# A gated cross-attention kernel on one Trainium2 core: a setup product split a second time, eight weight sums moved into the first quad, one buffer moved

## The chip, the cores and the metric

The kernel runs on one core of a Trainium2 chip. The metric is the time of one execution on the device in microseconds (us). The core's engines are named as the profile names them: PE is TensorE (matmul), PEld its weight loads, DVE is VectorE, ACT is ScalarE, POOL is GpSimd, SP is SyncE, which issues most DMAs. Each engine takes its own instructions in order and waits for the others by semaphores. PSUM, into which PE writes, has eight banks. SBUF is the working memory of all engines.

## The reference

`x` is (8, 1024, 1024), `ctx_1024` (the memory) is (8, 64, 512), all in float32. What is computed, with D = 1024:

```python
memory_proj = jnp.einsum('bme,de->bmd', memory, W_mem)
scores = jnp.einsum('bnd,bmd->bnm', hidden_states, memory_proj) / jnp.sqrt(jnp.float32(D))
attn = jax.nn.softmax(scores, axis=-1)
memory_context = jnp.einsum('bnm,bmd->bnd', attn, memory_proj)
gate_input = jnp.concatenate([hidden_states, memory_context], axis=-1)
gate = jax.nn.sigmoid(jnp.einsum('bnf,df->bnd', gate_input, W_gate) + b_gate)
fused = hidden_states + gate * memory_context
return _rmsnorm(fused, norm_w)
```

W_gate has two halves: W1 meets the rows of x, W2 meets memory_context. Since memory_context is attn times memory_proj, the kernel multiplies memory_proj by W2 once (the product "mg", 512 x 1024) and then attn by mg, so that the large product over all rows is x times W1 alone.

## The kernel before

**Strassen's products.** Each large product is done by Strassen's scheme in Winograd's form: the operands are cut into quarters, sums of quarters are formed, and seven products of quarters take the place of eight. The kernel numbers the seven products 1 to 7. The outer products run in the order 1, 6, 7, 5, 4, 2, 3 (`ORDER`, L604). In the main loop the scheme is used twice, one inside the other: each outer product is itself done by seven inner products, called A, B, C, D, A again, E and F (`outer_product`, L758). An inner product is two matmuls of 128x128 by 128x256, which the trace shows as four records.

**The rows.** x is worked in 16 quads of 512 rows (`NQ`). A quad has 49 slots (`SLOTS`), one for each inner product, and outer product number i of the order owns slots 7i to 7i + 6. The last two outer products of a quad are 2 (slots 35 to 41) and 3 (slots 42 to 48). Products 5, 4, 2 and 3 also carry the attn times mg part (`ext`, names pc and E, F).

**What is summed where.** The left sums of a quad, `outer_s` (DVE, 128x1024) and `inner_s` (POOL, four of 128x256 for each outer product, written to the tile L2), are made while the product before runs. The right sums come from W1 and are made once: `outer_sum` (L214, tiles t5, t6, t4) for products 5, 6 and 4, and `inner_sum` (L217, four of 128x512 for each outer product, tiles it1 to it7). The results are collected by `pre` on POOL (128x256 adds of u3 or u4, L797) and by `fin` on DVE (128x256 adds from PSUM, L803). `fin` of block n follows `pre` of block n.

**The banks.** An outer product uses five banks, and the next one takes them in rotated order (L898): its A gets the bank of the last product's C, its B that of D, its C that of A, its D that of E, its E that of B and F. So B of an outer product waits for the `fin` of D of the product before.

**The setup.** Before the first quad the memory is transposed and multiplied by W_mem (names pm, one step of Strassen), giving mp as the tiles m11 to m22. Then mg = mp times W2 follows in seven products of 256 x 512 by 512 x 512 (`mg_product`, L511: eight matmuls of 128x512 each, two banks; names pg) in the order 1, 6, 5, 2, 7, 4, 3. W2's quarters are b11 to b22, lists of four row chunks. The sums of mg are collected by DVE (`mg_sum`, L523) in c11, c12, c21 and c22, and stored to memory in DRAM (`store_mg`). Beside these products run: on POOL the sums of W2, then the inner sums of W1 for products 1, 7, 5, 6 and 4, with s3 (L540), s2 (L555) and `inner_s` of quad 0 between; on DVE the transposes of mp (`store_mp`, tiles mpq, stored to mgd by 16 DMAs), the transposes of xq, the outer sums of W1 and the sums of b21 (L569). The inner sums of products 2 and 3 are made by DVE in quad 0, at slots 3 to 6 and 22 to 25.

**Order.** Nearly every instruction is issued through `pin`, so each engine's queue has the order of the program text. Work that belongs to a later slot is put in by `at(slot, ...)`: what stands first in the program under one slot is issued first. `mid` puts work between A's second part and the `fin`s.

**Buffers.** The pool `const` has one buffer for each tag, `rot` two. A tile of the same tag has to wait until the accesses of the tile that held its buffer are over. Tag "l2" in `rot` is used by memq, then c21, then the L2 tiles. Tag "it2" in `const` is used by mpq of group 2 (`store_mp`, L492) and later by the inner sums of product 2; tags "it3" and "it4" likewise by mpq of groups 3 and 0 and by the inner sums of products 3 and 4.

These lines place the inner sums of products 2 and 3:

```python
for i, (o, n) in enumerate((o, n) for o in (2, 3) for n in range(4)):
    at((3, 4, 5, 6, 22, 23, 24, 25)[i], inner_sum, nc.vector, o, n)
```

Of the kernel before, what the change touches and what calls it, by code (L numbers as in the profile page):

```python
# [8 lines left out]
F32 = mybir.dt.float32  # L9
AF = mybir.ActivationFunctionType  # L10
ALU = mybir.AluOpType
# [4 lines left out]
P = 128  # L16
# [4 lines left out]
def tile_gated_cross_attention_rmsnorm(  # L21
# [42 lines left out]
    nc = tc.nc  # L64
# [8 lines left out]
    H = 512  # L73
    C = 256
# [4 lines left out]
    const = ctx.enter_context(tc.tile_pool(name="const", bufs=1))  # L79
# [3 lines left out]
    rot = ctx.enter_context(tc.tile_pool(name="rot", bufs=2))  # L83
    small = ctx.enter_context(tc.tile_pool(name="small", bufs=1))
# [4 lines left out]
    pin = tc.keep_in_program_order  # L89

    def mm(o, lhsT, rhs, start, stop):
        pin(nc.tensor.matmul(o, lhsT, rhs, start=start, stop=stop, skip_group_check=True))  # L92

    def tt(eng, o, a, b, op):
        pin(eng.tensor_tensor(o, a, b, op))  # L95
# [4 lines left out]
    def t4k(pool, shape, tag, name):  # L100
        return pool.tile(shape, F32, tag=tag, name=name)
# [5 lines left out]
    def chunks(t, n):  # L107

        return t.rearrange("p s e -> p (s e)").rearrange("p (m j) -> p j m", j=n)
# [26 lines left out]
    for k in range(KD):  # L136
        t = t4k(*((gpool, [P, D], "gate") if k < 7 else (apool, [P, D], "s4")), f"w2_{k}")
# [28 lines left out]
    def w1_place(o):  # L166

        if o in (5, 6, 4):
            outer_b[o] = const.tile([P, 4, H], F32, tag=f"t{o}", name=f"t{o}")
        inner_t[o] = const.tile([P, 3, 2, C], F32, tag=f"it{o}", name=f"it{o}")  # L170

    def w_op(o, s):
        if s >= T4:
            return inner_t[o][:, s - T4, :, :]
        k, n = {R11: (0, 0), R21: (1, 0), R12: (0, 1), R22: (1, 1)}[s]
        return outer_b[o][:, 2 * k : 2 * k + 2, n * C : (n + 1) * C]
# [37 lines left out]
    def outer_sum(o, a, b, k=slice(0, 4)):  # L214
        tt(nc.vector, outer_b[o][:, k], outer_b[a][:, k], outer_b[b][:, k], ALU.subtract)

    def inner_sum(eng, o, n):  # L217
        s, a, b = ((T1, R12, R11), (T2, R22, T1), (R12, R22, R12), (T4, R21, T2))[n]
        tt(eng, w_op(o, s), w_op(o, a), w_op(o, b), ALU.subtract)

    def inner_sums(eng, o):
        w1_place(o)
        for n in range(4):
            inner_sum(eng, o, n)
# [10 lines left out]
    def setup_bank(name):  # L235
        nonlocal setup_next
        tag = setup_banks[setup_next % 8]
        setup_next += 1
        return (ps_ctx if tag == "ctx" else ps).tile([P, H], F32, tag=tag, name=name)
# [8 lines left out]
    def pm_product(n, l, r, k_first=False):  # L248

        pgs = [setup_bank(f"pm{n}_{i}") for i in range(2)]  # L250
        if not isinstance(l, tuple):
            l = l[:, 0], l[:, 1]
        order = [(j, k) for j in range(KH) for k in range(2)]
        if k_first:
            order.sort(key=lambda jk: jk[1])
        for j, k in order:
            o = pgs[j // 2][:, (j % 2) * HM : (j % 2 + 1) * HM]
            mm(o, l[k][:, j, :], r[:, k, :], j % 2 == 0 and k == 0, k == 1)
        return pgs
# [34 lines left out]
    for k in range(2):  # L294
        pin(nc.scalar.copy(pw22[:, k], w22[:, k]))
    pgs = pm_product(2, w12, e21)
# [12 lines left out]
    pgs = pm_product(7, ps3, e12)  # L309
# [4 lines left out]
    b11, b12, b21, b22 = (  # L314
        [w2[h * KH + k][:, c * H : (c + 1) * H] for k in range(KH)]
        for h in range(2)
        for c in range(2)
    )
    t1, t2 = ([t[:, k, :] for k in range(KH)] for t in t_w2)

    def w2_sum(eng, o, a, b):
        for k in range(KH):
            tt(eng, o[k], a[k], b[k], ALU.subtract)
# [1 line left out]
    w2_sum(nc.gpsimd, t1, b12, b11)  # L325
    w2_sum(nc.gpsimd, t2, b22, t1)
    w2_sum(nc.gpsimd, b12, b22, b12)
    inner_sums(nc.gpsimd, 1)

    pgs = pm_product(3, ps4, e22)  # L330
    pm_sum(m21, m21, pgs)
# [8 lines left out]
    def transpose_x(q, t, half):  # L340

        key = q, t // 2, half
        if key not in A:
            A[key] = t4k(
                apool, [P, KH, 2 * P], f"a{t // 2 + 1}{half + 1}", f"a{t // 2 + 1}{half + 1}_{q}"
            )
        r = t % 2
        pin(
            nc.vector.transpose(  # L349
                A[key][:, :, r * P : (r + 1) * P],  # L350
                chunks(xq[q][:, 4 * t : 4 * t + 4, :], KD)[:, half * KH : (half + 1) * KH],
            )
        )

    def outer_s(q, n):
        a11, a12, a21, a22 = (A.get((q, r, h)) for r in range(2) for h in range(2))
        if n == 3:
            S[q, 3] = a21
            tt(nc.vector, a21, a11, a21, ALU.subtract)
            return  # L360
        s = S[q, n] = t4k(apool, [P, KH, 2 * P], f"s{n}", f"s{n}_{q}")
        if n == 1:
            tt(nc.vector, s, a21, a22, ALU.add)
        elif n == 2:
            tt(nc.vector, s, S[q, 1], a11, ALU.subtract)
        else:
            tt(nc.vector, s, a12, S[q, 2], ALU.subtract)
# [13 lines left out]
    def quarters(l):  # L381
        return l[:, 0:2, 0:P], l[:, 2:4, 0:P], l[:, 0:2, P:], l[:, 2:4, P:]
# [104 lines left out]
    def mp_step(eng, tag, pool, a, b, op):  # L487
        t = t4k(pool, [P, KH, HM], tag, f"mp_{tag}")
        tt(eng, t, a, b, op)
        return t  # L490
# [20 lines left out]
    def mg_product(n, l, r):  # L511
        pgs = []
        for t in range(2):
            pg = setup_bank(f"pg{n}_{t}")
            for k in range(KH):
                mm(pg, l[:, k, t * P : (t + 1) * P], r[k], k == 0, k == KH - 1)
            pgs.append(pg)
        return pgs

    def mg_tile(pool, tag, name):  # L520
        return t4k(pool, [P, 2, H], tag, name)

    def mg_sum(o, a, pgs):  # L523
        for t in range(2):
            tt(nc.vector, o[:, t, :], a[:, t, :], pgs[t], ALU.add)

    def store_mg(o, r, h):
        load(
            mgd[1, r * HM : (r + 1) * HM, h * H : (h + 1) * H].rearrange("(t p) e -> p t e", p=P),
            o,  # L530
        )

    s1 = mp_step(nc.vector, "s1", apool, m21, m22, ALU.add)
    s2 = mp_step(nc.vector, "s2", apool, s1, m11, ALU.subtract)
# [3 lines left out]
    outer_sum(7, 3, 7)  # L538
    w1_place(7)
    s3 = mp_step(nc.gpsimd, "junk", small, m11, m21, ALU.subtract)  # L540
    for n in range(4):
        inner_sum(nc.gpsimd, 7, n)
    c11 = mg_tile(rot, "u", "mg_c11")
    c12 = mg_tile(rot, "u", "mg_c12")
    c21 = mg_tile(rot, "l2", "mg_c21")
    c22 = mg_tile(small, "mg", "mg_c22")
    pgs = mg_product(1, m11, b11)
    for t in range(2):
# [4 lines left out]
    pgs = mg_product(6, s2, t2)  # L553
# [6 lines left out]
    pgs = mg_product(5, s1, t1)  # L560
    mg_sum(c12, c21, pgs)
    w1_place(6)
    outer_sum(6, 3, 5)
    for n in range(4):
        inner_sum(nc.gpsimd, 5, n)
    pgs = mg_product(2, m12, b21)
    mg_sum(c11, c11, pgs)
    store_mg(c11, 0, 0)
    w2_sum(nc.vector, b21, b21, t2)  # L569
    w1_place(4)  # L570
    outer_sum(4, 2, 6)
    for o in (6, 4):
        for n in range(4):
            inner_sum(nc.gpsimd, o, n)
    for t in range(2):
        transpose_x(0, t, 1)
    pgs = mg_product(7, s3, b12)
# [3 lines left out]
    pgs = mg_product(4, m22, b21)  # L581
    mg_sum(c21, c21, pgs)
    store_mg(c21, 1, 0)
    for t in (2, 3):
        transpose_x(0, t, 1)
    outer_s(0, 1)
    pgs = mg_product(3, s2, b22)
    mg_sum(c12, c12, pgs)
    store_mg(c12, 0, 1)
    outer_s(0, 2)  # L590
    load_mg(0)
# [5 lines left out]
    def at(slot, fn, *args):  # L597
        due.setdefault(slot, []).append(lambda: fn(*args))
# [45 lines left out]

    for o in (2, 3):
        w1_place(o)
    for i, (o, n) in enumerate((o, n) for o in (2, 3) for n in range(4)):
        at((3, 4, 5, 6, 22, 23, 24, 25)[i], inner_sum, nc.vector, o, n)
    slot = 0

    def step():
# [282 lines left out]
```

## Time and profile before

| what | us |
|---|---|
| median of 3 runs | 972.41 (972.2 to 973.52) |
| the profiled execution's own time | 972.56 |
| its span, first to last instruction | 970.8 |
| setup up to the first pg matmul | 0 to 33.44 |
| the seven products of mg (pg) | 33.44 to 81.5, PE busy throughout |
| quad 0, product 1 | from 81.35 |
| quad 0, product 6 | from 91.09 |
| quad 0, product 7 | from 97.45 |
| quad 0, product 5 | from 103.72 |
| quad 0, product 4 | from 111.89 |
| quad 0, product 2 | from 120.50 |
| quad 0, product 3 | from 128.67 |

The mean granted clock of TensorE over the span is 0.996 of full speed.

How to read the lines that follow in the prediction: a line of the timeline gives the start, the length in us, the engine, the line of the kernel, the operation and its tiles (output <- inputs), the shape, and how many instructions are merged; in brackets stands the idle time before it and who ended it. Most arithmetic is issued by two helpers, `mm` (L92) and `tt` (L95), so the tiles tell the operations apart and the lines don't. A line of the stretches gives the length and then busy us, with the number of instructions, of PE, PEld, DVE, ACT and POOL, the granted clock, the share of DMA and GB/s. A line of the waits gives the total, the number and the longest.

### The profile page before, as it was taken

The numbers are of one execution on the slowest core, as the hardware profiler recorded it, in microseconds if no ns is written. First come the engines' busy times: TensorE is split into PE (matmuls) and PEld (weight loads), VectorE is DVE, ScalarE is ACT, GpSimd is POOL, SyncE is SP. The second block draws the span as 40 slices with busy tenths as digits, with TensorE's granted clock in tenths as the row PEclk, the third lists the DMA queues.
The fourth block names the chain that finished last, engine by engine and source line by source line (L and its number), as shares of the span: only waits on it lengthen the run. The fifth ranks groups of instructions, "written<-read, shape, count | busy, mean of one in ns | idle before, by whom it ended". The sixth has DMA issues, their size and how long they took to land.

```text
span 970.8 us, 14402 instructions
## 1 busy us (share of the span) xinstructions
PE 959.5 (99%) x4986; PEld 774.9 (80%) x4986; DVE 818.4 (84%) x1482; ACT 328.5 (34%) x604; POOL 761.1 (78%) x889
## 2 busy tenths in 40 slices
PE   9999999999999999999999999999999999999995
PEld 8646878788888888788888888888887878888884
DVE  6988879879797988979797978979797978979787
ACT  2000234161423334161433324152333425152345
POOL 4997878778786978878786978878687878878692
PEclk9999999999999999999999999999999999999998
DMA  9856573482919374482918375381917465391712
GB/s 378 271 141 163 98 131 98 114 169 72 178 66 166 97 144 105 108 176 66 184 65 159 102 137 113 95 188 55 195 67 146 115 129 121 87 196 48 189 69 86
DMA packets 70919, 128.32 MB, mean 132 GB/s; under 512 B 12352, under 2 KB 49216, under 8 KB 70592
## 3 DMA queue, kind: packets, MB, share of 16 engines
q1 hardware_dynamic: 61520, 93.34, 37.0%
q0 software_dynamic: 9184, 33.56, 18.9%
q8 instruction: 39, 0.64, 0.3%
q10 hardware_dynamic: 144, 0.52, 0.1%
q14 instruction: 32, 0.26, 0.1%
HBM read 87.56 MB, written 41.68 MB: 133 GB/s over the span
## 4 chain that ended last, share of the span: by engine, by line
PE 98%; DVE 1%; issue 0%; ACT 0%; DVEq 0%
PE kA L92 20%; PE pc L92 12%; PE kE L92 11%; PE kD L92 10%; PE kF L92 10%; PE kB L92 10%; PE kC L92 10%; PE psT L92 6%; PE pg L92 5%; PE pm L92 3%; PE pz L92 0%; PE pa L443 0%; PE sc L417 0%; PE pt L196 0%; DVE gate L749 0%
## 5 line engine op out<-in xcount | busy, mean ns | idle before, releaser
L95 POOL TENSOR_TENSOR gate<-gate,u 128x256 f32<-128x256 f32 x336 | 287.5, 887 | 107.5 <-DVE u L95 107.5
L662 ACT ACTIVATE gate<-gate 128x512 f32<-128x512 f32 x128 | 80.5, 631 | 306.9 <-DVE gate L95 306.1
L349 DVE STREAM_TRANSPOSE a<-xq 128x512 f32<-128x512 f32 x128 | 137.9, 1099 | 2.7 <-POOL it L95 2.7
L95 POOL TENSOR_TENSOR l<-a 128x256 f32<-128x256 f32 x128 | 122.0, 953 | 21.6 <-PE kA L92 20.4
L92 PE MATMUL pc<-mg,attnT 64*128 64x256 f32 x512 | 127.5, 389 | 0.0
L92 PE MATMUL kB<-it,l 128*128 128x256 f32 x448 | 115.1, 379 | 0.2 <-DVE gate L95 0.2
L92 PE MATMUL kD<-it,l 128*128 128x256 f32 x448 | 115.0, 379 | 0.0
L92 PEld LDWEIGHTS pc<-mg,attnT 64*128 64x128 f32 x512 | 90.6, 186 | 29.9 <-issue 21.2
L691 DVE SCALAR_TENSOR_TENSOR gate<-gate,ss,nw_sb 128x512 f32<-128x512 f32 x120 | 110.6, 931 | 1.1
L95 POOL TENSOR_TENSOR l<-s 128x256 f32<-128x256 f32 x96 | 78.0, 813 | 36.1 <-PE kF L92 35.9
L92 PE MATMUL kA<-w,a 128*128 128x256 f32 x384 | 98.6, 379 | 0.0
L92 PEld LDWEIGHTS kB<-it,l 128*128 128x128 f32 x448 | 85.0, 190 | 12.1 <-DVE gate L95 0.6
L92 PEld LDWEIGHTS kD<-it,l 128*128 128x128 f32 x448 | 85.1, 190 | 11.6
L95 DVE TENSOR_TENSOR gate<-gate,pc 128x512 f32<-128x512 f32 x128 | 86.7, 678 | 0.4 <-ACT gate L662 0.4
L95 DVE TENSOR_TENSOR gate<-gate,kE 128x256 f32<-128x256 f32 x112 | 45.5, 419 | 47.1 <-PE kE L92 41.1
L92 PEld LDWEIGHTS kA<-w,a 128*128 128x128 f32 x384 | 71.7, 190 | 9.5 <-DVE s L95 0.2
L815 ACT COPY u<-kA 128x256 f32<-128x256 f32 x112 | 40.5, 361 | 110.3 <-PE kA L92 106.0
L92 PE MATMUL kE<-it,a 128*128 128x256 f32 x256 | 69.0, 392 | 0.0
L676 ACT ACTIVATE junk<-gate 128x1024 f32<-128x1024 f32 x60 | 63.5, 1058 | 10.5 <-DMA gate<-in_x 9.5
L92 PE MATMUL kA<-t,s 128*128 128x256 f32 x256 | 65.8, 379 | 0.0
L92 PE MATMUL kC<-w,l 128*128 128x256 f32 x256 | 65.7, 379 | 0.0
L92 PE MATMUL kF<-w,l 128*128 128x256 f32 x256 | 65.7, 379 | 0.0
(140 smaller groups left out, 2041.0 us busy)
## 6 DMA issues: line engine op xcount, KB each, us to landing
xq<-in_x SPq DMA_DIRECT2D x64, 512.0 KB, 10.3
gate<-in_x POOLq DMA_DIRECT2D x60, 512.0 KB, 8.1
out<-gate SPq DMA_DIRECT2D x60, 512.0 KB, 2.6
w<-in_w_gate_t SPq DMA_DIRECT2D x8, 512.0 KB, 10.0
w<-in_w_gate_t SPq DMA_DIRECT2D x2, 2048.0 KB, 17.1
mg<-mgd SPq DMA_DIRECT2D x16, 256.0 KB, 3.8
mpd<-mpT SPq DMA_DIRECT2D x4, 512.0 KB, 7.0
mgd<-mpq SPq DMA_DIRECT2D x16, 128.0 KB, 3.6
```

The costliest lines, as they stand in the source:

```text
L92: pin(nc.tensor.matmul(o, lhsT, rhs, start=start, stop=stop, skip_group_check=True))
L95: pin(eng.tensor_tensor(o, a, b, op))
L349: nc.vector.transpose(A[key][:, :, r * P : (r + 1) * P], chunks(xq[q][:, 4 * t : 4 * t + 4, :], KD)[:, half * KH : (half + 1) * KH],)
L662: pin(nc.scalar.activation(g, g, AF.Sigmoid))
L676: nc.scalar.activation(junk, O[q, t], AF.Square, accum_out=ss[:, t % 2 : t % 2 + 1])
L691: nc.vector.scalar_tensor_tensor(g[:, cols], g[:, cols], rstd[:, t % 2 : t % 2 + 1], nw_sb[:, cols], ALU.mult, ALU.mult,)
L815: pin(nc.scalar.copy(p1, kb["A"]))
```

## The change

Four things change.

- The last product of mp with W2, `mg_product(3, s2, b22)`, becomes `mg_nested`: the same product by a second step of Strassen. Its sums are four of b22's quarters for each of two row chunks (t1 to t4) and four of s2's (s1 to s4), twelve 128x256 operations on POOL. Seven products of 128x256 with two contraction steps follow on PE, in six banks. ACT copies the first, DVE makes u2, u3 and u4, POOL adds u3 or u4 to three blocks of c12, and DVE adds the four remaining banks. The sums lie in buffers it3 and it4.
- c21 moves from `rot`'s tag "l2" to `const`'s tag "it2".
- POOL's inner sums of products 5 and 4 leave the setup and come in quad 0 at slots 0, 0, 6, 6, 7, 7, 15, 15. The inner sums of product 1 on POOL come after s3's step.
- DVE's inner sums of products 2 and 3 move to slots 22 to 25 and 36 to 39.

```diff
     w2_sum(nc.gpsimd, b12, b22, b12)
-    inner_sums(nc.gpsimd, 1)
...
+    def mg_nested(eng, l, r, ts, ss, o):
+        l11, l12, l21, l22 = quarters(l)
+        s1_, s2_, s3_, s4_ = (ss[:, i] for i in range(4))
+        t1_, t2_, t3_, t4_ = (ts[i] for i in range(4))
+        lo, hi = slice(0, C), slice(C, H)
+        for k in range(2):
+            tt(eng, t1_[:, k, :], r[k][:, hi], r[k][:, lo], ALU.subtract)
+            tt(eng, t2_[:, k, :], r[2 + k][:, hi], t1_[:, k, :], ALU.subtract)
+            tt(eng, t3_[:, k, :], r[2 + k][:, hi], r[k][:, hi], ALU.subtract)
+            tt(eng, t4_[:, k, :], r[2 + k][:, lo], t2_[:, k, :], ALU.subtract)
+        tt(eng, s1_, l21, l22, ALU.add)
+        tt(eng, s2_, s1_, l11, ALU.subtract)
+        tt(eng, s3_, l11, l21, ALU.subtract)
+        tt(eng, s4_, l12, s2_, ALU.subtract)
+        yield
...
+        kb = [setup_bank(f"pn{i}")[:, :C] for i in range(6)]
+        ut = t4k(small, [P, 4, C], "junk", "mg_u")
+        p1_, u2, u3, u4 = (ut[:, i, :] for i in range(4))
+        def product(n, left_, right_, start=True):
+            for k in range(2):
+                mm(kb[n], left_[:, k, :], right_[k], start and k == 0, k == 1)
+        dst = [o[:, t, n * C : (n + 1) * C] for t in range(2) for n in range(2)]
+        def add(to, a, b):
+            tt(nc.vector, to, a, b, ALU.add)
+        product(0, l11, r11)
+        pin(nc.scalar.copy(p1_, kb[0]))
+        product(1, s2_, t2_)
+        add(u2, p1_, kb[1])
+        product(2, s3_, t3_)
+        add(u3, u2, kb[2])
+        for n in (3, 2):
+            tt(nc.gpsimd, dst[n], dst[n], u3, ALU.add)
+        product(3, s1_, t1_)
+        add(u4, u2, kb[3])
+        tt(nc.gpsimd, dst[1], dst[1], u4, ALU.add)
+        product(0, l12, r21, False)
+        product(4, l22, t4_)
+        product(5, s4_, r22)
+        yield
+        for n, b in ((0, 0), (3, 3), (2, 4), (1, 5)):
+            add(dst[n], dst[n], kb[b])
...
     s3 = mp_step(nc.gpsimd, "junk", small, m11, m21, ALU.subtract)
+    inner_sums(nc.gpsimd, 1)
...
-    c21 = mg_tile(rot, "l2", "mg_c21")
+    c21 = const.tile([P, 3, 2, C], F32, tag="it2", name="mg_c21")[:, :2]
+    c21 = c21.rearrange("p t k c -> p t (k c)")
...
     outer_sum(6, 3, 5)
-    for n in range(4):
-        inner_sum(nc.gpsimd, 5, n)
+    in_it3, in_it4 = (
+        const.tile([P, 3, 2, C], F32, tag=f"it{o}", name=f"mg_it{o}") for o in (3, 4)
+    )
+    ss3 = in_it4[:, 1:].rearrange("p a k c -> p (a k c)").rearrange("p (i k m) -> p i k m", i=4, k=2)
+    nested = mg_nested(
+        nc.gpsimd, s2, b22, [in_it3[:, 0], in_it3[:, 1], in_it3[:, 2], in_it4[:, 0]], ss3, c12
+    )
+    next(nested)
...
     outer_sum(4, 2, 6)
-    for o in (6, 4):
-        for n in range(4):
-            inner_sum(nc.gpsimd, o, n)
+    for n in range(4):
+        inner_sum(nc.gpsimd, 6, n)
...
     for t in (2, 3):
         transpose_x(0, t, 1)
+    next(nested)
     outer_s(0, 1)
-    pgs = mg_product(3, s2, b22)
-    mg_sum(c12, c12, pgs)
+    for _ in nested:
+        pass
     store_mg(c12, 0, 1)
...
+    for i, (o, n) in enumerate((o, n) for o in (5, 4) for n in range(4)):
+        at((0, 0, 6, 6, 7, 7, 15, 15)[i], inner_sum, nc.gpsimd, o, n)
     for i, (o, n) in enumerate((o, n) for o in (2, 3) for n in range(4)):
-        at((3, 4, 5, 6, 22, 23, 24, 25)[i], inner_sum, nc.vector, o, n)
+        at((22, 23, 24, 25, 36, 37, 38, 39)[i], inner_sum, nc.vector, o, n)
```

More of the change, by code (lines that the diff above doesn't have):

```diff
@@ L518, in mg_product @@
         return pgs
+    def mg_nested(eng, l, r, ts, ss, o):
[13 more added lines that the diff above has]
+        yield
+        r11, r22 = ([r[2 * h + k][:, n] for k in range(2)] for h, n in ((0, lo), (1, hi)))
+        r21 = [r[2 + k][:, lo] for k in range(2)]
+        t1_, t2_, t3_, t4_ = ([t[:, k, :] for k in range(2)] for t in (t1_, t2_, t3_, t4_))
+        kb = [setup_bank(f"pn{i}")[:, :C] for i in range(6)]
[24 more added lines that the diff above has]
+            add(dst[n], dst[n], kb[b])
     def mg_tile(pool, tag, name):
```

## The prediction

> **What bounds the kernel now.** I read the page's busy shares and chain first, then the waits of TensorE, then the stretches of the setup and the first quad, then each engine's timeline from 62 us to 131 us.
>
> ```profile
> PE 959.5 (99%) x4986; PEld 774.9 (80%) x4986; DVE 818.4 (84%) x1482; ACT 328.5 (34%) x604; POOL 761.1 (78%) x889
> ...
> PE 98%; DVE 1%; issue 0%; ACT 0%; DVEq 0%
> ```
> ```profile
> PE pz L92 <- DVE zeros L118: 1.2, 1, 1.2
> PE kB L92 <- DVE gate L95: 0.2, 1, 0.2
> ```
>
> TensorE is the bound: it is busy 959.5 of 970.8 us, and after its start it waits in the whole run only once, for 0.2 us. So all that can be won is TensorE work itself, and any new wait of TensorE is paid in full. That one wait is where the change reaches, in the first quad, so I look at who is loaded there.
>
> ```profile
> 62.13:81.98 19.85, 19.85 (x49) 9.03 (x48) 19.69 (x18) 0.00 (x0) 19.61 (x13) 1.00 0.21 79
> 81.98:87.64 5.66, 5.66 (x28) 4.72 (x28) 5.28 (x11) 0.74 (x2) 0.01 (x2) 1.00 0.60 179
> 87.64:103.59 15.95, 15.95 (x92) 13.03 (x91) 11.95 (x22) 3.00 (x8) 15.71 (x20) 1.00 0.87 152
> ```
>
> The columns are busy us of PE, PEld, DVE, ACT, POOL. POOL is full from 62.13 to 81.98 and from 87.64 to 103.59, with one hole of 5.65 us between. The next lines show both ends of this POOL queue, and what hangs on it.
>
> ```profile
> 73.46 1.27 POOL L95 TENSOR_TENSOR t<-t 128x512 f32<-128x512 f32 x1
> ...
> 79.73 2.25 POOL L95 TENSOR_TENSOR it<-t,it 128x512 f32<-128x512 f32 x1
> 87.64 0.91 POOL L95 TENSOR_TENSOR l<-s 128x256 f32<-128x256 f32 x1 [5.65 <-PE kF L92]
> ...
> 101.48 2.10 POOL L95 TENSOR_TENSOR gate<-gate,u 128x256 f32<-128x256 f32 x3
> ```
> ```profile
> 103.99 0.42 DVE L95 TENSOR_TENSOR gate<-gate,kF 128x256 f32<-128x256 f32 x1 [0.44 <-PE kF L92]
> ...
> 112.28 0.76 DVE L95 TENSOR_TENSOR gate<-gate,kD 128x256 f32<-128x256 f32 x2
> ```
> ```profile
> 113.09 1.13 PE L92 MATMUL kB<-it,l 128*128 128x256 f32 x4 [0.18 <-DVE gate L95]
> ```
>
> POOL's three `pre` adds of product 7 end at 103.59 (101.48 + 2.10). DVE's last `fin` of product 7 reads the third of them and starts at 103.99. From there DVE runs without a gap (attn_difference, four inner sums, u2 to u4, two transposes, the fins of product 5) to the kD fins, which end at 113.04, and TensorE's B of product 4, which reuses kD's bank, starts 0.05 us later. The chain POOL pre, DVE fin, DVE of product 5, TensorE has 0.4 us of slack at its head and none at its tail.
>
> **What the skill says.** "GPSIMD Engine Reference", section 1 Specifications: the SBUF interfaces are shared with VectorE, with contention where DVE has two SBUF inputs. The trace agrees: POOL's 128x512 sum takes 1.27 us alone (73.46) and 2.25 us beside DVE's 128x1024 outer_s (79.73). Section 4.1 Engine selection: two-input elementwise is about 2x slower on GpSimd. It agrees: 1.27 us against DVE's 0.68 us at 128x512. "PSUM — Partial Sum Buffer", section PSUM bank collisions: guard by bank, that is, a matmul waits for the reader of its bank. That is the 0.18 us wait at 113.09.
>
> **The change part by part.**
>
> TensorE. A product of mp with W2 takes 6.87 us (starts at 67.61, 74.48, 81.35). The nested one makes seven of 128x256 with two contraction steps each, 0.863 us apiece (four records; kA, kB, kC start 0.86 apart): 6.04 us. It removes 0.83 us, all of it on the path, if nothing it needs is late. Its sums come from POOL, in place of product 5's from 62.13 on: 12 x 0.69 = 8.3 us, plus 4.3 us beside DVE's four b21 sums (0.55 each, 1.71 - 1.27 and the issue) and its 128x2048 sum (2.1), so they end at 74.7, the tenth (s2_) at 73.3; the second nested product wants it at 75.3. Cover 2 us.
>
> POOL. Added in the setup: 8 sums of b22's quarters, 4 of s2's and 3 adds onto c12, all 128x256. Rows of that shape start 0.69 us apart (113.00, 113.69, 114.37): 15 x 0.69 = 10.35 us. Moved: 8 inner sums of products 5 and 4 (128x512) leave the setup and come at slots 0, 6, 7 and 15. They don't change the sum, since all eight stand ahead of product 7's `pre` in POOL's queue. W1's `inner_sums(1)` changes place with s3's step, both on POOL: s3 comes 5.0 us earlier, the sums 2.4 us later, and neither is needed before 60 us: nothing. The buffer of c21: rot's "l2" now serves only L2, so the wait of 5.65 us at 87.64 (for the F of product 1, which frees its buffer) goes, and slot 0's two sums fill the hole anyway. But outer_s(0,2) on DVE, 82.15 to 83.37, ran inside the hole; now POOL works beside it and loses about what 79.73 lost, 1.0 us. So the third `pre` of product 7 ends at 103.59 + 10.35 + 1.0 - 5.65 = 109.3. What is queued behind: L2's left sums for products 6, 7 and 5, b_gate's DMA, the `pre` adds of 6 and 7. Their fins on DVE free the banks for the next product's B and C, so TensorE stalls first at B of product 7, then at B of 5; all of that lies inside the final figure. DVE's last fin of 7 goes from 103.99 to about 109.35, +5.4. The DVE chain of product 5 is as long as before (four inner sums, now product 2's instead of 3's), so B of product 4 starts at 113.09 + 5.4 = 118.5. The 0.83 us won is swallowed: TensorE waits there whenever it came.
>
> DVE. In the setup two adds of 0.60 become seven of 0.33 (1.1 us more). dst[3], dst[2] and dst[1] wait for POOL's adds; behind them stand outer_s(0,2) and product 1's u2, which frees the bank for F of product 1. POOL: sums of product 6 to 80.7 (74.7 + 4 x 1.24 + 1.0 beside outer_s), adds to 82.8; so DVE's last add is done near 83.3, outer_s 84.7, u2 85.1; F wants the bank at 85.86. Covered by 0.8 us; if lost it lies in the same later wait. Slots 3 to 6 lose four inner sums (0.60 each), slots 22 to 25 swap them, slots 36 to 39, in product 2, get four new ones. There DVE is already without a gap from 120.77 to 128.5 (the four transposes, u's, pc's, fins). With four sums of 0.60 plus 0.5 us for a POOL sum that is under way at 121.7, the kD fin ends at 128.05 + 2.9 = 131.0; B of product 3 wants its bank at 129.53: a wait of 1.5 us. Bounds: 0.5 us (some of the 2.4 us falls into small gaps) to 2.9 us (DVE queues behind POOL as e did at 97.86, where a 0.4 us operation took 1.7). After it DVE idles 2.4 us at 137.4, so the backlog ends.
>
> c21 in it2. That buffer also holds mpq of group 2, whose stores land late (the longest of these is 9.6 us, the first issued at 43.3). DVE's add into c21 at 48.71 would wait to about 53.9. DVE idles 2.7 us there anyway for xq, so it is 2.4 us late afterwards; behind it are xq's transposes and b21's sums, which end at 67.74 and are wanted for the fourth chunk at 70.2. Hidden, at 0; bounds 0 and 2.4 us. c12's store and mg's load come up to 3 us later than 82.3 and 85.4; b_gate's DMA on POOL waits for mg and now issues at 98, and xq(1) behind it on SP lands near 102, wanted at 115: nothing.
>
> Sum: +5.4 (product 4) + 1.5 (product 3) = +6.9. Profiled span 970.8 + 6.9 = 977.7; around it lie 972.56 - 970.8 = 1.76, so 979.5, and the median is 0.15 under the profiled run: 979.3.
>
> The POOL term's bounds: 9.0 - 5.65 - 0.4 = 2.9 (adds at 0.6, no new contention) to 10.35 + 3.0 - 5.65 - 0.4 = 7.3 (two more DVE operations that cost POOL 1.0 each).
>
> **The rivals.**
> 1. POOL's backlog reaches TensorE, as above: 979.3, own range 975.8 (2.9 and 0.5) to 982.6 (7.3 and 2.9). Chance 0.70. For it: POOL's two full windows. Against: POOL's spans are rough.
> 2. Not slower. POOL absorbs the 15 adds. It decides at the third `pre` of product 7: if the net growth of POOL's queue stays under the 0.4 us of slack there, that is if adds plus contention cost at most 6.05 us, which the hole and the slack cover, where I count 11.35. Then the end is 972.41 - 0.83 = 971.6 up to 973.1 with the wait in product 3. For it: POOL's operations beside DVE hold long waits that could overlap. Against: alone they also take 0.69. Chance 0.12.
> 3. Half of it: POOL is late by 2 us only, because DVE's idle moments move away from POOL's sums, or the wait in product 3 is all that remains: 973 to 976, about 974.5. Chance 0.10.
> 4. More: c21's wait for its buffer delays DVE by 2.4 us and b21's sums come late for their product, and that lag goes on through product 1 into POOL: 979.3 + 2.4 to 4.5 = 981.7 to 983.8. Chance 0.08.
>
> **How the numbers follow.** This kernel's runs lie 0.14% apart, so 0.2% (1.9 us) is what can be told from no change. Case 2 is below 974.4 and mostly above 970.5: same 0.09, faster 0.03. A third of case 3 is within 974.4: same 0.12 in all, slower 0.85. The range 974.5 to 983.5 leaves out case 2, a third of case 3 and a little of case 4, about 0.18.
>
> **What would show it.** Right: no idle POOL between 82 and 88; the last `pre` of product 7 near 109; waits of kB in products 7, 5, 4 and 3, with B of product 4 about 5 us later than 113.09 and B of product 3 another 1.5 later; seven nested products in 6.0 us. Wrong: kB of product 4 at 112 to 113, TensorE without waits but the span near 970; or a wait of mg_c for mpq's DMA that TensorE feels in the setup.

## The result: 0.66% slower, and the profile after

| | before | after |
|---|---|---|
| median, us | 972.41 (972.2 to 973.52, 5 runs) | 978.75 (978.34 to 979.15, 5 runs) |
| ratio | | 1.0066, 95% interval 1.0054 to 1.0077 |
| span of the profiled execution | 970.8 | 977.0 |
| quad 0, product 1 (first kA) | 81.35 | 79.94 |
| product 6 | 91.09 | 89.88 |
| product 7 | 97.45 | 96.25 |
| product 5 | 103.72 | 108.11 |
| product 4 | 111.89 | 116.30 |
| product 2 | 120.50 | 125.37 |
| product 3 | 128.67 | 134.99 |
| quad 1, product 1 | 140.44 | 146.79 |

TensorE comes to the first quad 1.41 us earlier, and leaves it 6.35 us later. From there on the two run alike: the spans differ by 6.2. By stage: product 7 lasts 11.86 us instead of 6.27 (+5.59), and between the start of product 4 and that of product 3 it loses another 1.91 (18.69 against 16.78).

The page after, busy shares and chain:

```profile
PE 961.1 (98%) x4998; PEld 777.4 (80%) x4998; DVE 818.5 (84%) x1487; ACT 329.2 (34%) x605; POOL 775.0 (79%) x904
...
PE 90%; POOL 4%; DVE 3%; DMA 1%; issue 1%; ACT 0%; SPq 0%; DVEq 0%; POOLq 0%
```

POOL and DVE have entered a chain that was TensorE's for 98%. The waits of TensorE after (total, number, longest):

```profile
PE kB L92 <- DVE gate L95: 2.9, 2, 2.3
...
PE kD L92 <- DVE u L95: 0.8, 1, 0.8
PE pa L442 <- DVE e L95: 0.6, 1, 0.6
PE kC L92 <- POOL l L95: 0.4, 1, 0.4
```

Before there was one such wait, of 0.2 us. These waits are not all that TensorE loses. Of the 5.59 us lost in product 7, 3.31 are waits (2.26 at B, 0.44 at C, 0.61 at pa). The other 2.28 are matmuls that run longer: TensorE's busy time in product 7 (the first figure after the length) is 8.55 us instead of 6.27, with a mean granted clock (behind POOL's figure) of 0.86 instead of 1.00. The first line is before, the second after:

```profile
97.45:103.72 6.27, 6.27 (x32) 5.49 (x30) 4.73 (x10) 1.83 (x5) 6.19 (x10) 1.00 0.45 74
96.25:108.11 11.86, 8.55 (x31) 6.13 (x30) 7.82 (x11) 1.84 (x5) 11.70 (x16) 0.86 0.43 69
```

In the stretch in which C runs, right behind the waits at B and C, the granted clock was 0.58. The prediction has no such term. In the kernel after, the end doesn't hang on it: it lies ahead of B of product 4, and this B still waits 0.63 us for DVE.

The same three stretches as before, and the new one up to the end of product 7's `pre`:

```profile
62.13:81.98 19.85, 19.85 (x66) 12.11 (x65) 19.71 (x25) 0.75 (x2) 19.62 (x18) 1.00 0.21 80
81.98:87.64 5.66, 5.66 (x34) 4.24 (x34) 4.66 (x9) 0.37 (x1) 5.50 (x6) 1.00 0.46 146
87.64:103.59 15.95, 13.25 (x66) 10.10 (x63) 10.33 (x13) 1.53 (x4) 15.79 (x16) 0.93 0.91 163
103.59:109.15 5.56, 4.95 (x22) 3.83 (x21) 4.16 (x8) 1.47 (x4) 5.48 (x9) 0.89 0.00 0
```

POOL (the fifth busy figure) is full in all four; the hole of 5.65 us is gone. What fills it, on POOL's timeline:

```profile
79.44 3.08 POOL L95 TENSOR_TENSOR mg_c<-mg_c,mg_u 128x256 f32<-128x256 f32 x3
82.48 1.27 POOL L95 TENSOR_TENSOR it<-t 128x512 f32<-128x512 f32 x1
83.82 2.14 POOL L95 TENSOR_TENSOR it<-t,it 128x512 f32<-128x512 f32 x1
85.92 0.73 POOL L95 TENSOR_TENSOR l<-s 128x256 f32<-128x256 f32 x1
...
88.79 2.25 POOL L95 TENSOR_TENSOR t<-t 128x512 f32<-128x512 f32 x1
...
101.43 1.51 POOL L95 TENSOR_TENSOR t<-t 128x512 f32<-128x512 f32 x1
102.65 1.51 POOL L95 TENSOR_TENSOR it<-t,it 128x512 f32<-128x512 f32 x1
...
107.05 2.10 POOL L95 TENSOR_TENSOR gate<-gate,u 128x256 f32<-128x256 f32 x3
```

The three adds onto c12, then two of product 5's inner sums at slot 0, L2 for product 6 from 85.92 (87.64 before), four more sums from 88.79, two at 101.43, and the `pre` adds of product 7 end at 107.05 + 2.10 = 109.15. DVE's last `fin` of product 7 follows at 109.19:

```profile
100.73 4.40 DVE L95 TENSOR_TENSOR e<-e,den 128x256 f32<-128x256 f32 x1
...
109.19 0.42 DVE L95 TENSOR_TENSOR gate<-gate,kF 128x256 f32<-128x256 f32 x1 [0.26 <-POOL gate L95]
```

And TensorE, at B of products 7 and 4 and at the attn times mg part of product 2:

```profile
99.53 1.13 PE L92 MATMUL kB<-it,l 128*128 128x256 f32 x4 [2.26 <-DVE gate L95]
...
117.96 1.13 PE L92 MATMUL kB<-it,l 128*128 128x256 f32 x4 [0.63 <-DVE gate L95]
...
132.53 0.70 PE L92 MATMUL kD<-mg,attnT 64*128 64x256 f32 x2 [0.76 <-DVE u L95]
```

The nested products start at 73.90 and end where product 1 starts, at 79.94: 6.04 us.

### The profile page after: what moved, and what is told of

It reads as the page before. It is cut to its first block, busy times and chain, and to the rows that moved or that the text cites. A ratio compares the mean times of both kernels' runs of the same rounds, so it can differ in the third digit from the quotient of the medians.

```text
span 977.0 us, 14451 instructions
## 1 busy us (share of the span) xinstructions
PE 961.1 (98%) x4998; PEld 777.4 (80%) x4998; DVE 818.5 (84%) x1487; ACT 329.2 (34%) x605; POOL 775.0 (79%) x904
## 4 chain that ended last, share of the span: by engine, by line
PE 90%; POOL 4%; DVE 3%; DMA 1%; issue 1%; ACT 0%; SPq 0%; DVEq 0%; POOLq 0%
PE kA L92 19%; PE pc L92 12%; PE kE L92 11%; PE kD L92 10%; PE kF L92 10%; PE kB L92 10%; PE kC L92 10%; PE psT L92 6%; PE pm L92 2%; DMA xq<-in_x 1%; POOL it L95 1%; POOL mg_it L95 1%; POOL l L95 1%; PE pz L92 0%; DVE e L95 0%
## 5 line engine op out<-in xcount | busy, mean ns | idle before, releaser
L751 DVE SCALAR_TENSOR_TENSOR gate<-gate,ss,nw_sb 128x512 f32<-128x512 f32 x120 | 108.3, 912 | 1.1
```

Of the source, the lines that this page charges most:

```text
L751: nc.vector.scalar_tensor_tensor(g[:, cols], g[:, cols], rstd[:, t % 2 : t % 2 + 1], nw_sb[:, cols], ALU.mult, ALU.mult,)
```

## The experiments

The theory put to the test: what stands in POOL's queue ahead of product 7's `pre` adds sets their end (T below), T sets DVE's stretch of product 5, and this sets B of product 4; four DVE sums in product 2 add some 1.4 us. Each kernel was timed beside the kernel before on the same chip (972.2 to 972.3 there).

| run | median, us | ratio (95%) | T | B of 4 | B of 4 less T | span |
|---|---|---|---|---|---|---|
| before | 972.4 | | 103.59 | 113.09 | 9.5 | 970.8 |
| after | 978.75 | 1.0066 (1.0054 to 1.0077) | 109.15 | 117.96 | 8.8 | 977.0 |
| e1 plain product | 976.37 | 1.0039 (1.0026 to 1.0052) | 105.86 | 114.70 | 8.8 | 973.7 |
| e2 sums earlier | 979.74 | 1.0073 (1.0059 to 1.0086) | 109.56 | 119.06 | 9.5 | 978.1 |
| e3 c21 back | 978.95 | 1.0067 (1.0054 to 1.0079) | 108.69 | 118.17 | 9.5 | 977.2 |
| e4 DVE sums back | 979.83 | 1.0077 (1.0065 to 1.0090) | 111.05 | 120.53 | 9.5 | 978.0 |
| e5 no b22 sums | 979.92 | 1.0081 (1.0067 to 1.0095) | 109.89 | 118.71 | 8.8 | 977.7 |
| e6 before plus 4 | 972.31 | 1.0001 (0.9993 to 1.0009) | 103.41 | 112.89 | 9.5 | 970.6 |
| e7 before plus 15 | 981.67 | 1.0096 (1.0083 to 1.0110) | 112.25 | 122.16 | 9.9 | 979.7 |
| e8 product 3's sums in product 4 | 977.75 | 1.0056 (1.0043 to 1.0069) | 108.95 | 118.44 | 9.5 | 976.0 |
| e9 nested alone | 982.16 | 1.0101 (1.0087 to 1.0115) | 113.62 | 123.08 | 9.5 | 981.4 |
| e10 no c12 adds | 977.27 | 1.0049 (1.0035 to 1.0062) | 107.64 | 117.31 | 9.7 | 976.5 |
| e11 sums spread | 974.92 | 1.0032 (1.0021 to 1.0042) | 102.82 | 113.34 | 10.5 | 973.0 |
| e12 sums spread again | 972.32 | 0.9999 (0.9990 to 1.0007) | 103.46 | 112.89 | 9.4 | 970.8 |

**The two halves apart.** e1 takes the nested product out of the kernel after and keeps the moves; e9 puts the nested product alone into the kernel before (its sums in it2 and it3).

```diff
# e1, from after
-    nested = mg_nested(...)
-    next(nested)
...
+    pgs = mg_product(3, s2, b22)
+    mg_sum(c12, c12, pgs)
# e9, from before
+    nested = mg_nested(...)
+    next(nested)
     for n in range(4):
         inner_sum(nc.gpsimd, 5, n)
...
-    pgs = mg_product(3, s2, b22)
-    mg_sum(c12, c12, pgs)
```

> Kernel after, with only the nested product undone: mg_product(3, s2, b22) again, all moved sums and c21's buffer as after. Theory A (GpSimd's fifteen added 128x256 operations, 10.35 us, are what makes product 7's pre adds late): the third pre of product 7 ends near 99 to 100 instead of 109.15, no wait in products 7, 5 and 4; TensorE gets 0.83 us more work back and the 1.4 us of product 2 stay: span 970.8 + 1.4 = 972.2, about 973.9 us. Theory B (the eight moved inner sums make it late by standing between product 6's and 7's work): still 977 to 979.

> Kernel before, with the nested product as the only change: its sums in it2 and it3, c21 in l2, every inner sum where it was before. GpSimd then makes the sums of products 5, 6 and 4 between the nested sums and the adds onto c12, which so start near 89 us; DVE and product 1's F wait for them. Theory A3 (the end of product 7's pre adds is what counts, and the nested product and the moved sums are two ways to the same delay): L2's sums for product 6 start near 93, the third pre of product 7 ends at 109 to 110, about 978; no wait in product 2. If the moved sums are to blame: 971.6 to 973.

Neither half is free: the moves alone cost 4.1 us of time (T 2.3 later), between the two expectations for e1, and the nested product alone 10.0, well above the expected 978. In e1 POOL now idles in the setup, and the sums that would fit there stand in the quad. Its timeline:

```profile
72.91 1.27 POOL L95 TENSOR_TENSOR it<-t,it 128x512 f32<-128x512 f32 x1
82.77 0.73 POOL L95 TENSOR_TENSOR l<-s 128x256 f32<-128x256 f32 x1 [8.59 <-DVE s L95]
```

L2 of product 6 can't start before DVE's outer_s ends, however empty POOL's queue is. In e9 the wait sits elsewhere. The waits of TensorE in e9, and the POOL line behind them:

```profile
PE kF L92 <- DVE u L95: 8.6, 1, 8.6
```
```profile
90.33 2.09 POOL L95 TENSOR_TENSOR mg_c<-mg_c,mg_u 128x256 f32<-128x256 f32 x3
```

The c12 adds stand behind the sums of products 5, 6 and 4 in POOL's queue and come at 90.33 instead of 79.44. DVE's c12 adds wait for them, and behind those stands product 1's u2, which frees the bank of F. Product 1 lasts 20.96 us instead of 9.74, which is 2.6 us more than the wait: its matmuls run longer here too, with a mean granted clock of 0.76. So in e9 TensorE is late from product 1 on, and T is late with it.

**The sums moved only part of the way.** e2 makes product 5's sums in the setup, ahead of product 6's, and product 4's at slot 0.

```diff
-    for n in range(4):
-        inner_sum(nc.gpsimd, 6, n)
+    for o in (5, 6):
+        for n in range(4):
+            inner_sum(nc.gpsimd, o, n)
...
-    for i, (o, n) in enumerate((o, n) for o in (5, 4) for n in range(4)):
-        at((0, 0, 6, 6, 7, 7, 15, 15)[i], inner_sum, nc.gpsimd, o, n)
+    for i, (o, n) in enumerate((o, n) for o in (4,) for n in range(4)):
+        at((0, 0, 0, 0)[i], inner_sum, nc.gpsimd, o, n)
```

> Kernel after, with product 5's inner sums on GpSimd back in the setup (ahead of product 6's) and product 4's all at slot 0; the nested product stays. Theory A (the amount of work ahead of product 7's pre adds counts, not its place): their end stays near 109, the time stays at 978.7 within 1.0. Theory B (the place of the eight sums counts): 971.6 to 974.

T is 0.4 us later (109.56) and the time 1.0, at the edge of what the first theory allowed. The wait has moved from product 7 to F of product 1 (4.2 us, again for DVE's u), and product 1 lasts 7.3 us longer than before, at a mean granted clock of 0.80. All eight sums stood ahead of product 7's `pre` in both; so far that is what the prediction's sum of the queue says.

**The added operations.** e6 and e7 add 4 and 15 subtractions of b22's quarters (128x256), whose results nothing uses, to POOL's queue at the end of the setup of the kernel before. e5 leaves out of the kernel after the eight sums of b22's quarters (the nested product then takes the raw quarters, so c12 is another matrix). e10 leaves out the three adds of u3 and u4 onto c12.

```diff
# e6, e7, from before
+    extra = t4k(small, [P, C], "extra", "extra")
+    for i in range(4):   # 15 in e7
+        tt(nc.gpsimd, extra, b22[i % 4][:, :C], b22[i % 4][:, C:], ALU.subtract)
# e5, from after
-            tt(eng, t1_[:, k, :], r[k][:, hi], r[k][:, lo], ALU.subtract)
...
-            tt(eng, t4_[:, k, :], r[2 + k][:, lo], t2_[:, k, :], ALU.subtract)
# e10, from after
-            tt(nc.gpsimd, dst[n], dst[n], u3, ALU.add)
...
-        tt(nc.gpsimd, dst[1], dst[1], u4, ALU.add)
```

> Kernel before, with 4 more 128x256 subtractions on GpSimd (2.8 us) into a tile that nothing reads, at the end of the setup's queue. They lie in the hole of 5.65 us: unchanged within 0.5. If GpSimd's work is paid for everywhere: 2.8 us slower.

> Kernel before, with 15 such subtractions (10.35 us) at the same place, as many as the change adds. Theory A: the hole takes 5.65, the slack at product 7 0.4, DVE's outer_s and four inner sums now meet a busy GpSimd (up to 1.0 + 2.2): between 4.3 and 7.5 us slower, the third pre of product 7 at 108.3 to 111.5, with no change of the product, the buffer or any slot.

> Kernel after, with the eight sums of b22's quarters left out: the nested products multiply b22's quarters themselves, so that mg is another matrix, and TensorE's work is unchanged. GpSimd loses 8 x 0.69 = 5.5 us. Theory A in its first form (every us taken from GpSimd comes back): third pre of product 7 at 103.7, about 974. Theory A2 (GpSimd can't run ahead of outer_s(0,2), which it needs near 82.7, so that only the excess over that comes back, as in the kernel with the plain product): pre near 105.9, 3.0 us faster than after, about 975.7.

> Kernel after, with the three adds of u3 and u4 onto c12 left out on GpSimd (2.1 us), so three blocks of c12 lack them. Theory A3 (these adds wait for DVE's u3 near 79.2 and hold up GpSimd's queue, so that sums ahead of them are free and work behind them is not): L2's sums for product 6 start 1.5 us earlier (bound then by outer_s(0,2)), 1.5 us faster than after, about 977.2. Theory A in its first form: 2.1 faster. If work ahead of product 6 is all free: 978.7.

Four operations vanish in the hole. Fifteen took 16.10 us (1.07 each, not 0.69), pushed L2 of product 6 to 97.20, and cost 9.4 us, more than the 4.3 to 7.5 expected:

```profile
81.14 16.10 POOL L95 TENSOR_TENSOR extra<-w 128x256 f32<-128x256 f32 x15
```

TensorE waited 7.2 us at B of product 6, and this product lasted 10.1 us longer than before, at a mean granted clock of 0.69. In e5 eight operations of 0.69 less gave nothing back, where both expectations had 3 us or more. POOL's timeline in e5 shows why:

```profile
73.12 1.28 POOL L95 TENSOR_TENSOR it<-t,it 128x512 f32<-128x512 f32 x1
80.23 3.07 POOL L95 TENSOR_TENSOR mg_c<-mg_c,mg_u 128x256 f32<-128x256 f32 x3 [5.83 <-DVE mg_u L95]
83.26 1.26 POOL L95 TENSOR_TENSOR it<-t 128x512 f32<-128x512 f32 x1
```

The c12 adds wait for u3, which TensorE and DVE have only then (mg_u starts at 79.24 on DVE, 78.44 after), and hold all that is queued behind them: POOL idles 5.83 us where the sums were. T is 0.74 us later than after, about as much as DVE's mg_u. e10 is the counterpart: without those three adds POOL goes from product 6's sums at once to slot 0's, and of the 2.1 us that they take alone (2.09 in e9) 1.5 come back in T, and 1.5 in the median time; POOL then waits 1.41 us for DVE's outer_s ahead of L2 of product 6, which hides the rest. In the profiled execution of e10, the slowest of its five (978.24), B of product 4 starts only 0.65 us earlier than after and waits for nothing: there TensorE comes last, held in product 7 by DVE's e, an operation that the last section comes back to:

```profile
PE pa L442 <- DVE e L95: 2.2, 1, 2.2
```

So an operation ahead of that wait costs nothing until the queue ahead lasts past it, and one behind it makes T later, up to what the next wait hides.

**The moved buffer and DVE's moved sums.** e3 puts c21 back into "l2". e4 puts DVE's sums back to slots 3 to 6 and 22 to 25, e8 moves product 3's from product 2 into product 4.

```diff
# e3
-    c21 = const.tile([P, 3, 2, C], F32, tag="it2", name="mg_c21")[:, :2]
-    c21 = c21.rearrange("p t k c -> p t (k c)")
+    c21 = mg_tile(rot, "l2", "mg_c21")
# e4, e8: slots of DVE's sums of products 2 and 3
-(22, 23, 24, 25, 36, 37, 38, 39)
+(3, 4, 5, 6, 22, 23, 24, 25)     # e4
+(22, 23, 24, 25, 32, 32, 33, 34) # e8
```

> Kernel after, with c21 back in the two-buffer tag l2. Theory A: DVE's wait of 5.67 us at 48 us for mpq's stores shrinks to the 2.7 us for xq, but it is hidden either way, and slot 0's sums cover the wait for product 1's F: 978.7 within 0.7. Theory C (c21's wait delays DVE and so everything behind it): 976.3 or less. Theory D (the buffer is what fills GpSimd's hole): slower by up to 1.5.

> Kernel after, with DVE's inner sums of products 2 and 3 back at slots 3 to 6 and 22 to 25. Theory A: the 1.2 us wait in product 2 goes, but the four sums at slots 3 to 6 now meet a busy GpSimd and cost it up to 0.55 us each: between 977.3 (no contention) and 979.5 (all four). If the slots of these sums cost nothing: 978.7.

> Kernel after, with DVE's four inner sums of product 3 at slots 32, 32, 33, 34 in place of 36 to 39: DVE idles there 2.8 us in four pieces. Theory A: the wait in product 2 (about 1.4 us) goes and nothing takes its place: 977.3. If the sums only move the lag to product 4: 978.7.

e3 can't be told from after. In e8 TensorE's wait for kD in product 2 is gone (A of product 2 to A of product 3 takes 8.29 us, 9.62 after), for 1.0 us of time. In e4 it is gone too (8.16), but the sums at slots 3 to 6 run beside POOL's L2 of product 6 (1.18 and 1.06 us an operation, 0.73 after), T is 1.9 us later, and the time 1.1 above after, just outside the expected range.

**Another place for the sums.** e11 and e12 keep the whole nested product and c21's buffer and change only the inner sums of products 5, 4, 2 and 3: their slots, and which of the two engines makes them. (In the lists: slot, product, n.)

```diff
# e11
+        (nc.gpsimd, ((0, 5, 0), (0, 5, 1), (22, 5, 3), (22, 4, 2), (27, 4, 3), (37, 3, 0), (41, 3, 1), (41, 3, 2), (44, 3, 3))),
+        (nc.vector, ((3, 4, 0), (4, 4, 1), (5, 5, 2), (22, 2, 0), (23, 2, 1), (32, 2, 2), (33, 2, 3))),
# e12
+        (nc.gpsimd, ((0, 5, 0), (0, 5, 1), (23, 4, 2), (27, 4, 3))),
+        (nc.vector, ((3, 4, 0), (4, 4, 1), (5, 5, 2), (6, 5, 3), (22, 2, 0), (23, 2, 1), (24, 2, 2), (32, 2, 3),
+                     (32, 3, 0), (33, 3, 1), (34, 3, 2), (46, 3, 3))),
```

> Kernel after, with the inner sums of products 5, 4, 2 and 3 spread anew: on GpSimd two of product 5 at slot 0 and one at 22, two of product 4 at 22 and 27, product 3's at 37, 41, 41, 44; on DVE two of product 4 and one of product 5 at slots 3 to 5, product 2's at 22, 23, 32, 33. The six sums of 1.24 us that stand between product 6's left sums and product 7's pre adds go, three on DVE cost GpSimd up to 0.55 each. Theory A3: the third pre of product 7 ends near 103.5, no wait above 0.5 us in products 7, 5, 4 and 2, and the 0.83 us of the nested product is left over: 970.5 to 972.5. If the nested product's sums themselves are what is paid: still 976 or more.

> After with the sums of products 5, 4, 2 and 3 spread once more: GpSimd makes only four in the quad (two of product 5 at slot 0, one of product 4 at slots 23 and 27), VectorE the other twelve (slots 3 to 6, 22 to 24, 32 to 34 and 46). Theory (what stands in POOL's queue between its wait for the nested u3 and the third pre of product 7 sets B of product 4, and each engine's other work decides the rest): POOL carries 2.5 us there as in the spread run before, so the third pre of product 7 ends at 103 to 104, product 7 lasts 6.3 us, B of product 4 starts near 113; as no pair of POOL sums now stands at slot 22 and none in product 2 or 3, VectorE's attnT difference isn't held and the wait of product 3 goes. 971.5 to 973.5, the 0.83 us of the nested product won and about as much given back. If the holding of VectorE's operation with two SBUF inputs comes back somewhere else in the quad: 974 to 976. If a nested product in this place costs time whatever the sums do (rival): 975 or more with the third pre of product 7 later than 105.

e11 brings T back to 102.82 and is still 2.7 us above before, outside both of its expectations. DVE's attnT difference, 1.12 us before, takes 3.93 there:

```profile
103.31 3.93 DVE L95 TENSOR_TENSOR attnT<-attnT 64x256 f32<-64x256 f32 x1
```

POOL's timeline in e11 at the same time:

```profile
103.45 1.59 POOL L95 TENSOR_TENSOR it<-t,it 128x512 f32<-128x512 f32 x1
104.69 1.58 POOL L95 TENSOR_TENSOR t<-t 128x512 f32<-128x512 f32 x1
105.91 1.03 POOL L95 TENSOR_TENSOR l<-a 128x256 f32<-128x256 f32 x1
107.02 0.80 POOL L95 TENSOR_TENSOR l<-l,a 128x256 f32<-128x256 f32 x1
```

DVE's u behind it frees the bank that the attn times mg part needs. The waits of TensorE in e11 show both losses, this one (at kF) and one for a sum of product 3 that POOL makes too late:

```profile
PE kB L92 <- POOL it L95: 1.2, 1, 1.2
PE kF L92 <- DVE u L95: 1.0, 1, 1.0
```

e12 takes POOL's sums from slot 22 and out of products 2 and 3. The `pre` adds of product 7 then end at 101.36 + 2.10 = 103.46:

```profile
101.36 2.10 POOL L95 TENSOR_TENSOR gate<-gate,u 128x256 f32<-128x256 f32 x3
```

The waits left to TensorE in it:

```profile
PE pz L92 <- DVE zeros L118: 1.2, 1, 1.2
PE kD L92 <- DVE u L95: 0.7, 1, 0.7
```

972.32 us, ratio 0.9999 with an interval from 0.9990 to 1.0007: the 6.3 us of the change are gone, with every part of the nested product in place. Of the lead over before of 1.48 us at product 1 (79.87 against 81.35) nothing is left at product 4 (112.02 against 111.89): T is where it was, and DVE's u4 of product 5 with it, so TensorE waits for kD. No version measured here is faster than before.

## Why the prediction was right, step by step

- **The sum.** +6.9 us forecast, +6.2 in the span. The third `pre` of product 7 ends at 109.15 (109.3 forecast), B of product 4 starts 4.87 later than before (5.4), and from B of product 4 to product 3 another 1.45 are lost (1.5). The term that was too large is B of product 4. DVE's stretch from the last fin of product 7 to this B was to stay as long as before, 9.10 us (103.99 to 113.09); it took 8.77 (109.19 to 117.96), with the attnT difference at 0.57 us and not the 1.12 of before.
- **The chain.** For the kernel after it is as forecast: the last fin of product 7 starts 0.04 us after T, DVE runs from there without a gap, and B of product 4 waits 0.63 us for it. The traces of e1, e3, e4, e5, e6 and e8 show the same (B waits 0.63 to 0.65). The near-constant distance of T and B in the table is no proof for the other runs. In e2, e7, e9 and e10 TensorE was held earlier: the last fin comes 0.7 to 1.1 us after T and waits for F of product 7, and B of product 4 waits for nothing, so T is late there together with TensorE and not ahead of it. In e11 and e12 B doesn't wait either. What is lost up to this B stays lost: before's 970.8, plus the shift of B of product 4, plus about 1.4 where DVE's product 3 sums stand in product 2, gives every span within 0.7 us but e11's, which has a loss of its own in product 3.
- **What fills POOL.** Here the step "They don't change the sum" for the eight moved sums, with all of the cost in the 15 added operations, doesn't hold. e5 takes eight of the fifteen away and gains nothing; e1 takes all fifteen away and still loses 2.3 us of T. It is the wait for u3 that divides the queue. In after POOL reaches that wait at 79.44, about when u3 is there, so counting operations and counting from the wait meet in one figure; that the total came out at 109.3 is to this extent luck. So is the size of its parts: the twelve sums of the nested product were to take 12.6 us from 62.13; they took 14.3 from 60.08 and so ended at 74.37, near the 74.7 forecast. Counted from what stands behind the wait: L2 of product 6 starts 1.7 us earlier (85.92 against 87.64), and six inner sums now stand between it and T, where 23.2 us pass instead of 15.95: T is 5.6 later. That the sums' place and engine are paid, and not the nested product itself, e12 shows: with only two of these sums on POOL ahead of T, and the rest later or on DVE, the change costs nothing. Which of the two, the place or the engine, brings how much was not tried apart.
- **The first stalls.** B of product 7 waits as forecast (2.26 us). B of product 5 doesn't: TensorE is held before it, at C of product 7 for L2 (0.44) and at pa for DVE's e (0.61), and its matmuls run 2.28 us longer between these waits.
- **Product 2's DVE sums.** The size was right and e8 confirms the cause; the place was not B of product 3 (no wait there) but the attn times mg part of product 2, which needs the bank that u4 frees. DVE reached u4 at 132.10.
- **Nested products, c21, c12.** 6.04 us as forecast, swallowed. TensorE was another 0.6 us earlier at the start of product 1, also swallowed; this is not the change's doing, as e6, whose code is before's up to there, has product 1 at 80.62, 0.73 earlier than before. c21's add on DVE waited to 53.83 (53.9 forecast), and e3 shows that the buffer costs nothing in either place. DVE's last c12 add ended at 82.97 (83.3 forecast), but F of product 1 was not covered by 0.8 us: u2 ended at 85.16 and F started at 85.22.
- **The rivals.** Not slower, decided by POOL's absorbing the adds: refuted for this placement, and reached by e12 with another. Half of it: e11 lies there and e1 just above, after doesn't. The wait of c21: refuted by e3.

## What to carry to other kernels

In this kernel the price of an operation added to POOL's in-order queue depended on which side of the next wait it stood: ahead of it, the wait hid it (e5, e6); behind it, it made what follows later, up to the slack of the wait after that (e10, 1.5 of 2.1 us). So before moving helper sums out of a full stretch, look for the consumer that is late next on the same queue, and put only as much ahead of it as it had slack. A saving of TensorE time before such a consumer was worth nothing here until the consumer itself came earlier. And count TensorE's busy time beside its waits: in e7 a wait of 7.2 us lengthened product 6 by 10.1.

## What the runs showed of the hardware that was not expected

A DVE operation with two SBUF inputs was held here while POOL's operations followed one another without a gap, with no wait between the two in the trace. `e<-e,den` (128x256) took 0.60 us in e2 and e9, 1.71 before, 4.40 after; the attnT difference took 0.57 after and 3.93 in e11. In each of the five traces named below, the held DVE operation ends 0.3 us after the start of the first gap of some 0.08 us in POOL's queue, where POOL reads what its operation just before wrote: in e11 POOL's gap is at 106.94 to 107.02, and attnT ends at 107.24; after, the gap is at 104.83 to 104.92, and e ends at 105.13. That the two contend when DVE has two SBUF inputs is what the Trainium skill ("GPSIMD Engine Reference", section 1 Specifications) states, and the trace agrees: DVE operations with one input from PSUM stayed at 0.42 us beside the same POOL work. That the gap releases it was read from five traces (before, after, e1, e11, e12) and not tried by itself.

The other thing is the granted clock behind TensorE's waits. Behind waits of 2.3 us and more it fell: over the whole product in which the wait lay, its mean was 0.86 after (product 7), 0.80 in e2, 0.76 in e9 (product 1 in both) and 0.69 in e7 (product 6). In e1, with one wait of 1.6 us in product 7, it stayed at 1.00. How long a wait it takes was not tried.
